# One branch at the end in place of two, one-pass group norms, and a layer that starts on half of the images, in a four-layer fp32 network on one core

## The chip, the core and the metric

The kernel runs on one core of a Trainium2 chip, in one launch. The metric is the device time of a launch in microseconds (us), as the median over several runs. TensorE is written PE, VectorE DVE, ScalarE ACT, GpSimd POOL and SyncE SP, as in the profile.

## The reference

The input x has 8 images of 384 channels and 32x32 pixels, all in fp32. Four layers follow each other, each of the form x + f(gn(x)), where gn is a group norm with 32 groups of 12 channels and without weights:

```python
def _gn(v, G=32, eps=1e-5):
    g = v.reshape(B_, G, C_ // G, H_, W_)
    m = jnp.mean(g, axis=(2, 3, 4), keepdims=True)
    s = jnp.var(g, axis=(2, 3, 4), keepdims=True)
    return ((g - m) / jnp.sqrt(s + eps)).reshape(v.shape)
...
# layer 0: q, k, v = 1x1 projection(gelu(batch norm(3x3 depthwise(x))))
attn = softmax(einsum('bhcn,bhcm->bhnm', q, k) * scale)        # 8 heads of 48 channels
out = bn(einsum('oc,bchw->bohw', w_out, einsum('bhnm,bhcm->bhcn', attn, v)))
# layer 1: 4 experts
scores = softmax(x_flat @ gate_w + gate_b, -1)
top_v, top_i = jax.lax.top_k(scores, K)                        # K = 2
top_w = softmax(top_v, -1)
present = (top_i[:, :, None] == jnp.arange(e)[None, None, :]).any(0)
coef = einsum('ke,kbhw->ebhw', present, top_w)
hdn = relu(einsum('bchw,edc->ebdhw', x, w1) + b1)
out = einsum('ebohw,ebhw->bohw', einsum('ebdhw,eod->ebohw', hdn, w2) + b2, coef)
# layer 2: 7x7 depthwise convolution with reflected edges, plus bias
# layer 3: three branches of small MLPs and 1x1, 3x3, 5x5 depthwise convolutions,
#          weighted by a softmax over pooled features, then a 384x384 projection
```

`present` says whether an expert was chosen by any pixel of any image at all, once as first and once as second choice. Where every expert was, coef is the same for all experts at a pixel: the two softmax weights add up to 1, so layer 1 is the plain sum over all four experts.

## The kernel before

**Tiles.** Channels lie on the 128 partitions in three tiles (NC = 3, "ct" 0 to 2); an image has N = 1024 pixels, in two halves of HF = 512, and each half in two of QF = 256. A matmul in fp32 appears in the trace as two instructions. A group norm over 12 channels crosses partitions: `over_group` (L237) multiplies the moments per channel with block matrices gmat, 7 of them (each output tile gets shares from its neighbouring tiles). `gn_steps` does this twice: the mean first, then DVE centres (L248 to L251), then the variance; `rsqrt` (L204, L205) raises to the power -0.5 on POOL, and L255 makes the offset. Scale and offset are applied by ACT (L270).

**Stages.** First layer 0's norm, convolutions, batch norms and projections; then attention, image by image (`attention`, scores L655, exponentials L662, output L674, projection L730). The kernel uses exponentials without subtracting a maximum, and notes in `shift_needed` whether a bound on the scores was exceeded. After it comes a branch (L845, L846): if so, `attention(True)` does all again with a maximum. All engines wait for it.

Then `bn_coefs` (L276 to L280) and the moments of layer 0's sum (L865 to L881), worked out from those of its parts without reading the sum, and the norm of all 8 images at once (L237 on 24 columns). s1, t1 (L883, L884) are kept.

**Layer 1** is `experts()`. Image 0's residual r is loaded (L1002, from layer 0's output in DRAM; L1003 the input xr), as are w1, one transfer per expert (L1030), and w2; DVE makes r (L1009), ACT normalises (L270, `normed`). For each image and half, 12 pairs of expert and hidden tile: three matmuls (L1147) and relu on ACT (L1151). Then the product with w2, in a scheme that trades matmuls for additions: `sums` (L1064) on DVE, 24 products of four experts each (L1071), whose results DVE adds to r (L1085, L1087). During the next image's first half the pieces of `next_layer` run, one every expert or two: the finished r is saved (L918, eight transfers on SP), its statistics taken (L210, L266), `gn_steps`, and for each ct `pass_on`: ACT normalises, DVE transposes (L902), POOL adds the mirrored edges (L903, L904) and SP saves (L928). `logits` (L1114, L1125) and the choice of experts go between too, and the last of it, `absent`, decides a second branch (L1371, L1372): `experts_by_token` would do layer 1 again with the choice per pixel. `attention` and layers 2 and 3 have their order on PE, ACT, DVE written out by hand (`manual_schedule`); in `experts()` a scheduler sets it. SP's transfers are placed by the scheduler everywhere.

**Layer 2** treats a depthwise 7x7 convolution as banded 64x64 matmuls over columns, with the images side by side (L1619): for each ct eight c, for each c two e (parities), each with 28 matmuls over all 8 images (64x256). Its weights are loaded (`load_weights`, L1344), their edges folded by POOL (L1348) and spread by ACT into a banded form (`next_weights`, L1361). xt, the transposed input of one ct for all images, is loaded ahead: ct 0 of images 0 to 6 at the end of `experts()`, ct 1 at L1449; image 7's ct 0 goes straight into it. After a pair of c, ACT takes the results from PSUM (L310). Layer 3 (L1586 and on) ends with the projection (L2001 to L2012), DVE's sum with the residual (L2016) and the output's transfers (L2023).

**Memory.** Pools are stacks: what is opened after a closing lies where the closed pool lay, and its first writers wait for the old pool's last users. Before, `wp` (gate weights) lies below `zs` (moments of the batch norm); `ew` (weights of layer 1) and then `er` (r, transposed tiles) come where zs was.

Of the kernel before, what the change touches and what calls it, by code (L numbers as in the profile page):

```python
# [18 lines left out]
P = 128  # L19
# [117 lines left out]
def conv_mixer_kernel(ctx: ExitStack, tc: tile.TileContext, a: dict, out: bass.AP):  # L137
# [79 lines left out]
    def gn_steps(mv, pool_ps, tag="gn", order="A"):  # L217
# [34 lines left out]
        yield  # L252
# [5 lines left out]
        yield s, t  # L258

# [34 lines left out]
    mvx = early.tile([P, 2, NC, B], FP, name="mvx")  # L294
    s1, t1 = (early.tile([P, NC, B], FP, name=f"{n}1") for n in "st")
# [20 lines left out]
    with (  # L316
# [27 lines left out]
        with tc.tile_pool(name="cps", bufs=2, space=PSUM, reuse_waits="tile") as cps:  # L344
# [70 lines left out]
            for n, (ct, v, u) in enumerate(groups):  # L415
# [21 lines left out]
                if n == 1:  # L437
                    norm = gn_steps((mvx[:, 0], mvx[:, 1]), slot0)
                    next(norm)
# [35 lines left out]
    wpool = ExitStack()  # L475
    wp = wpool.enter_context(tc.tile_pool(name="wp", bufs=1))
    zpool = ExitStack()
    zs = zpool.enter_context(tc.tile_pool(name="zs", bufs=1))
    zst = zs.tile([P, NC, 2 * B, 6], FP, name="zst")
    mvz = zs.tile([P, 2, NC, 2 * B], FP, name="mvz")  # L480
    mvxh = zs.tile([P, 2, NC, 2 * B], FP, name="mvxh")
    zx = zs.tile([P, NC, 2 * B], FP, name="zx")
    bn_gbo = load(zs, "bn_gbo")
    shift_needed = zs.tile([1, 1], mybir.dt.int32, name="shift_needed")

    def attention(shifted):

        with tc.tile_pool(name="aw", reuse_waits="tile", bufs=1) as aw, tc.tile_pool(  # L490
            name="ay", reuse_waits="tile", bufs=2
        ) as ay, tc.tile_pool(
            name="sc", reuse_waits="tile", bufs=3, space=PSUM
        ) as scp, tc.tile_pool(name="av", reuse_waits="tile", bufs=2, space=PSUM) as avp:
            pw_v = load(aw, "pw_v")
            w_out = load(aw, "w_out")
            if shifted:

                pws = pp0.tile([P, 2 * NC * NC, P], FP, tag="pw", name="pws")
                pw_q = pws[:, : NC * NP].rearrange("p (c k) n -> p c k n", k=NP)  # L500
                nc.sync.dma_start(out=pw_q, in_=a["pw_qs"])
                pw_k = load(aw, "pw_ks")
                ones_row = aw.tile([P, 1], FP, name="ones_row")
                nc.gpsimd.memset(ones_row, 0.0)
                nc.gpsimd.memset(ones_row[0:1, :], 1.0)
                nc.gpsimd.memset(ones_row[64:65, :], 1.0)
            else:
                pw_q, pw_k = pw[:, 0], pw[:, 1]

                own = aw.tile([P, 3], FP, name="own")
                nc.gpsimd.memset(own, 1.0)
                for o, base, sign in ((1, 15, -1), (2, -16, 1)):
                    for q in range(4):
                        v = own[32 * q : 32 * q + 32, o : o + 1]
                        nc.gpsimd.affine_select(
                            out=v, in_=v, compare_op=ALU.is_ge, fill=0.0, base=base,
                            pattern=[[0, 1]], channel_multiplier=sign,
                        )  # L520
                nc.gpsimd.tensor_copy(own[32:64, 0:1], own[32:64, 1:2])
                nc.gpsimd.tensor_copy(own[64:96, 0:1], own[64:96, 2:3])
            chk = aw.tile([P, B * 2 * NP], FP, name="chk")
            if shifted:
                mx = pws[:, NC * NP : NC * NP + 4]
                nc.gpsimd.memset(mx, 0.0)
            ys, kTs, qTs, atts, xs = {}, {}, {}, {}, {}

            def fetch(b):
                ys[b] = []  # L530
                for v in range(3):
                    if b == 0 and v in ys0 and not shifted:
                        ys[b].append(ys0[v])
                        continue
                    pool = pp0 if v < 2 else ay
                    y = pool.tile([P, NC, N], FP, tag=f"y{v}", name=f"y{v}", bufs=1)
                    nc.sync.dma_start(out=y, in_=raw[v][b])
                    ys[b].append(y)

            def activate(b, v):  # L540
                for ct in range(NC):
                    i = v * NC + ct
                    y = ys[b][v][:, ct, :]
                    affine(y, y, bn_s[:, i : i + 1], bn_t[:, i : i + 1], AF.Gelu)

            def two_banks():
                return scp.tile([P, 2, HF], FP, tag="sc", name="sc")

            def project(w, pair, y):
                ps = two_banks()  # L550
                for h in range(2):
                    for ct in range(NC):
                        nc.tensor.matmul(  # L553
                            ps[:, h, :], lhsT=w[:, ct, pair, :],
                            rhs=y[:, ct, h * HF : (h + 1) * HF],
                            start=ct == 0, stop=ct == NC - 1,
                        )
                return ps.rearrange("p h n -> p (h n)")

            def spread(w, y, o, own, act=False, between=None):  # L560


                for t in range(NC):
                    ps = project(w, t, y)
                    if between and t == NC - 1:
                        between()
                    to = [[(0, None)], [(32, 1), (64, 2)], [(96, None)]][t]
                    affine(o[:, t, :], ps, own[:, 0:1] if own is not None else 1.0, 0.0)
                    moves = [(o[64:96, t, :], 32, 2)]
                    moves += [(o[p : p + 32, NP - 1, :], 64, i) for p, i in to]  # L570
                    for d, p, i in moves:
                        if act:
                            nc.scalar.copy(d, ps[p : p + 32, :])
                        elif own is None or i is None:
                            nc.vector.tensor_copy(d, ps[p : p + 32, :])
                        else:
                            nc.vector.tensor_scalar(
                                d, ps[p : p + 32, :], own[p : p + 32, i : i + 1], None, ALU.mult
                            )

            def project_k(b):
                kT = kTs[b] = ay.tile([P, NP, N], FP, tag="kT", name="kT", bufs=1)
                if not shifted:
                    return spread(pw_k, ys[b][1], kT, None, b == 0)
                for pair in range(NP):
                    affine(kT[:, pair, :], project(pw_k, pair, ys[b][1]), 1.0, ones_row)

            def project_q(b, between=None):
                qT = qTs[b] = ay.tile([P, NP, N], FP, tag="qT", name="qT", bufs=1)
                if not shifted:  # L590
                    return spread(pw_q, ys[b][0], qT, own, between=between)
                for pair in range(NP):
                    ps = project(pw_q, pair, ys[b][0])
                    nc.vector.tensor_scalar(qT[:, pair, :], ps, HD**-0.5, None, ALU.mult)

            vTs = []

            def project_v(b):
                y = ys[b][2]
                if not vTs:  # L600
                    vTs.append(ay.tile([P, N // P, HEADS * 64], FP, tag="vT", name="vT", bufs=1))
                    nc.gpsimd.memset(vTs[0], 1.0)
                vT = vTs[0]
                for m0 in range(0, N // P, 2):
                    ps = two_banks()
                    for m in range(2):
                        for ct in range(NC):
                            nc.tensor.matmul(  # L608
                                ps[:, m, :C], lhsT=y[:, ct, (m0 + m) * P : (m0 + m + 1) * P],
                                rhs=pw_v[:, ct, :], start=ct == 0, stop=ct == NC - 1,  # L610
                            )
                    nc.vector.tensor_copy(
                        vT[:, m0 : m0 + 2, :].rearrange("p m (a c) -> p m a c", c=4)[:, :, :, 0:3],
                        ps[:, :, :C].rearrange("p m (a c) -> p m a c", c=3),
                    )

            def shift(b):

                qT, kT = qTs[b], kTs[b]
                for h in range(2):  # L620
                    for pair in range(NP):
                        for n in range(4):
# [24 lines left out]

            def scores(b, h, pair, g):

                es = []  # L650
                for m in range(g * GM, (g + 1) * GM):
                    sc = two_banks()
                    for s in range(2):
# [1520 lines left out]
```

## Time and profile before

| | us |
|---|---|
| median of 3 runs | 3244.41 (3243.41 to 3246.69) |
| profiled execution | 3250.0 |
| its span | 3248.1 |
| PE busy | 3048.7 |
| DVE busy | 1674.7 |
| ACT busy | 1189.1 |
| POOL busy | 257.9 |
| mean granted PE clock | 0.974 of full speed |

The profile is of one execution; its times are from the start of its span. In a row of a group the columns are: source line, engine, operation, what is written and from what, shape and count, then busy time, mean duration of one in ns, and the engine's idle time before them with what ended most of it. "PEld" is PE's weight load, which overlaps its matmuls; "SPq" and "DVEq" are an engine's own queue, as at a branch. Slices show an engine's busy share of 1/40 of the span in tenths. A timeline line has start, duration, engine, source line, operation, count, and in brackets the idle time ahead of it and what ended it; equal neighbours are drawn together. The rows of the page that cost most PE time are attention and layer 1:

```profile
L1147 PE MATMUL ph<-xn,w 128*128 128x512 f32 x1152 | 507.8, 597 | 0.7 <-ACT xn L270 0.7
L655 PE MATMUL sc<-qT,kT 64*128 64x512 f32 x2048 | 477.6, 603 | 10.4 <-ACT e L662 10.4
L674 PE MATMUL av<-e,vT 128*64 128x512 f32 x2048 | 467.7, 598 | 0.0
```

### The profile page before, as it was taken

The numbers are of one execution on the slowest core, as the hardware profiler recorded it, in microseconds if no ns is written. First come the engines' busy times: TensorE is split into PE (matmuls) and PEld (weight loads), VectorE is DVE, ScalarE is ACT, GpSimd is POOL, SyncE is SP. The second block draws the span as 40 slices with busy tenths as digits, with TensorE's granted clock in tenths as the row PEclk, the third lists the DMA queues.
The fourth block names the chain that finished last, engine by engine and source line by source line (L and its number), as shares of the span: only waits on it lengthen the run. The fifth ranks groups of instructions, "written<-read, shape, count | busy, mean of one in ns | idle before, by whom it ended". The sixth has DMA issues, their size and how long they took to land. (4 is left out here: it accounts for less than half of the span.)

```text
span 3248.1 us, 42048 instructions
## 1 busy us (share of the span) xinstructions
PE 3048.7 (94%) x17628; PEld 1615.6 (50%) x17628; DVE 1674.7 (52%) x2536; ACT 1189.1 (37%) x1340; POOL 257.9 (8%) x408
## 2 busy tenths in 40 slices
PE   5987999999999999999997999999999997987999
PEld 3774334343433333343432576676666665655544
DVE  6996344445444544444444454553654654257174
ACT  3644553535354453535442212212212111446520
POOL 3331000000000000000002100000000000111400
PEclk9998999999999999999998999999999997998999
DMA  5887001011101111020014021121121113777665
GB/s 215 288 277 263 36 31 71 23 61 42 61 22 59 43 40 61 22 80 23 13 35 153 14 57 44 62 75 34 55 82 28 42 43 105 276 258 237 224 219 198
DMA packets 87992, 322.76 MB, mean 99 GB/s; under 512 B 13304, under 2 KB 15696, under 8 KB 83560
## 3 DMA queue, kind: packets, MB, share of 16 engines
q1 hardware_dynamic: 64168, 251.71, 22.7%
q10 hardware_dynamic: 13488, 35.81, 3.5%
q0 software_dynamic: 10128, 32.36, 2.9%
q8 instruction: 143, 2.34, 0.3%
q14 instruction: 65, 0.53, 0.1%
HBM read 211.65 MB, written 111.53 MB: 99 GB/s over the span
## 5 line engine op out<-in xcount | busy, mean ns | idle before, releaser
L662 ACT ACTIVATE e<-sc 128x1024 f32<-128x1024 f32 x512 | 483.1, 1029 | 544.0 <-PE sc L655 543.6
L1147 PE MATMUL ph<-xn,w 128*128 128x512 f32 x1152 | 507.8, 597 | 0.7 <-ACT xn L270 0.7
L655 PE MATMUL sc<-qT,kT 64*128 64x512 f32 x2048 | 477.6, 603 | 10.4 <-ACT e L662 10.4
L674 PE MATMUL av<-e,vT 128*64 128x512 f32 x2048 | 467.7, 598 | 0.0
L1151 ACT ACTIVATE hs<-ph,b 128x512 f32<-128x512 f32 x192 | 131.9, 687 | 605.6 <-PE ph L1147 552.7
L1147 PEld LDWEIGHTS ph<-xn,w 128*128 128x128 f32 x1152 | 217.3, 191 | 260.8 <-issue 256.7
L655 PEld LDWEIGHTS sc<-qT,kT 64*128 64x128 f32 x2048 | 185.7, 186 | 297.4 <-issue 228.9
L674 PEld LDWEIGHTS av<-e,vT 128*64 128x64 f32 x2048 | 135.5, 136 | 316.5 <-issue 316.5
L553 PE MATMUL sc<-y,pw 128*128 128x512 f32 x576 | 252.1, 599 | 8.0 <-ACT y L270 8.0
L425 PE MATMUL ps<-xt,wx 64*64 64x256 f32 x3456 | 198.2, 388 | 41.0 <-DVE xt L361 22.0
L690 DVE LOAD_MASK_SELECT sm<-av x64 | 0.9, 14 | 424.1 <-PE av L674 424.1
L692 DVE RECIPROCAL inv<-sm 128x512 f32<-128x512 f32 x64 | 214.6, 3353 | 2.2
L1085 DVE TENSOR_TENSOR r<-r,p 128x256 f32<-128x256 f32 x416 | 155.3, 416 | 104.0 <-PE p L1071 103.1
L425 PEld LDWEIGHTS ps<-xt,wx 64*64 64x64 f32 x3456 | 155.5, 137 | 82.6 <-issue 44.9
L1619 PE MATMUL ps<-xt,wx 64*64 64x256 f32 x2688 | 158.2, 394 | 30.7 <-SPq L1372 18.5
L553 PEld LDWEIGHTS sc<-y,pw 128*128 128x128 f32 x576 | 109.8, 192 | 149.8 <-issue 138.6
L1071 PE MATMUL p<-hs_sum,wsum 128*128 128x256 f32 x768 | 173.7, 379 | 0.5 <-DVE r L1085 0.5
L1064 DVE TENSOR_TENSOR hs_sum<-hs 128x768 f32<-128x768 f32 (+1 forms) x96 | 60.7, 687 | 206.9 <-ACT hs L1151 206.9
L1071 PEld LDWEIGHTS p<-hs_sum,wsum 128*128 128x128 f32 x768 | 145.8, 190 | 20.8 <-DVE r L1085 1.1
L1619 PEld LDWEIGHTS ps<-xt,wx 64*64 64x64 f32 x2688 | 109.4, 138 | 78.3 <-issue 26.0
L608 PE MATMUL sc<-pw_v,y 128*128 128x384 f32 x384 | 127.5, 493 | 13.0 <-ACT y L270 13.0
L1064 DVE TENSOR_TENSOR hs_sum<-hs,hs_sum 128x768 f32<-128x768 f32 (+1 forms) x192 | 138.2, 775 | 1.1
(302 smaller groups left out, 3322.6 us busy)
## 6 DMA issues: line engine op xcount, KB each, us to landing
raw<-y SPq DMA_DIRECT2D x72, 512.0 KB
y<-raw SPq DMA_DIRECT2D x24, 1536.0 KB
x<-x SPq DMA_DIRECT2D x23, 608.0 KB
xt<-x SPq DMA_DIRECT2D x23, 608.0 KB
w<-in_w ACTq DMA_DIRECT2D x36, 384.0 KB
xn<-in_x SPq DMA_DIRECT2D x24, 512.0 KB
x<-in_x SPq DMA_DIRECT2D x16, 768.0 KB
z<-z POOLq DMA_DIRECT2D x16, 768.0 KB, 4.3
```

Of the source, the lines that this page charges most:

```text
L425: nc.tensor.matmul(ps[64 * d : 64 * d + 64, 2 * i + e, cc], lhsT=w[r, 12 * cc + 6 * e + 3 * d + k, :], rhs=xt0s[ct][r, 16 * d + 4 * u + 2 ...
L553: nc.tensor.matmul(ps[:, h, :], lhsT=w[:, ct, pair, :], rhs=y[:, ct, h * HF : (h + 1) * HF], start=ct == 0, stop=ct == NC - 1,)
L655: nc.tensor.matmul(sc[:, s, :], lhsT=kTs[b][r, pair, m * P : (m + 1) * P], rhs=qTs[b][r, pair, h * HF : (h + 1) * HF], start=True, stop=True,)
L662: nc.scalar.activation(e, sc, AF.Exp, scale=1.0 if shifted else HD**-0.5)
L674: nc.tensor.matmul(av[64 * s : 64 * s + 64, :], lhsT=vTs[0][:, m, c0 : c0 + 64], rhs=e[:, s, :], start=m == 0, stop=m == N // P - 1,)
L692: nc.vector.reciprocal(inv, sm)
L1064: nc.vector.tensor_add(rows_of(o, hs, s), rows_of(i, hs, s), rows_of(j, hs, s))
L1071: nc.tensor.matmul(ps[:, :QF], lhsT=block(w)[:, e], rhs=rows_of(x, hs, e), start=e == 0, stop=e == E - 1,)
L1085: nc.vector.tensor_tensor(out=o, in0=o, in1=ps[:, :QF], op=op)
L1147: nc.tensor.matmul(ph, lhsT=w1[:, e, ct, dc * P : (dc + 1) * P], rhs=xns[b, h][:, ct, :], start=ct == 0, stop=ct == NC - 1,)
L1151: nc.scalar.activation(hs[:, dc, e], ph, AF.Relu, bias=b1[:, e, dc : dc + 1])
L1619: nc.tensor.matmul(ps[64 * d : 64 * d + 64, 2 * i + e, c % 2], lhsT=w[r, d * K7 + k, :], rhs=by_slot(xts[ct])[r, 16 * d + column(c, e, 2), ...
```

## The change

Everything behind layer 0's projections is put into a function `layers(again, ...)`. Both branches go. `bounded` (of attention) and the presence of the experts are multiplied into one flag `repeat`, and at the very end one branch calls `layers(True, ...)`, which does attention with the maximum and layer 1 per pixel, and all behind. For it, layer 0's statistics xst are saved to DRAM, and mvx and the group means of x (gmx) stay in a lasting pool.

A group norm of layers 1 and 2 no longer finds the mean before the variance. The group mean of its input is guessed from known numbers (`ref`: the mean of the layer's input plus a constant of the biases, gmy); DVE forms the moments about that reference, and one pass of 7 matmuls yields both. In layer 1's start the power is taken in two parts, image 0 first.

`experts()` now has its order written by hand, POOL included. The pool er is opened ahead of ew. Four weight tiles of layer 2 are spread at its end (a fourth, wx4, lies in er). Image 7's norm comes in two parts: moments of ct 0 and 1 and group block 0, then the rest. Between them PE does layer 2's c = 0 and 1 on images 0 to 3, and after them on images 4 to 7. PSUM's two tiles of four banks are one pool on each side.

```diff
+    def centred(o, mean, var, ref):
+        nc.vector.tensor_sub(o[:, :, 0], mean, ref)
+        nc.vector.tensor_mul(o[:, :, 1], o[:, :, 0], o[:, :, 0])
+        nc.vector.tensor_add(o[:, :, 1], o[:, :, 1], var)
+
+    def from_moments(own, ps, ref, s, t, gm, firsts=None):
+        c, n = ps.shape[1], ps.shape[3]
+        both, sq = (
+            own.tile([P, c, n], FP, tag=f"fm_{k}", name=f"fm_{k}") for k in "ab"
+        )
+        nc.vector.tensor_copy(both, ps[:, :, 0])
+        nc.vector.tensor_mul(sq, both, both)
+        nc.vector.scalar_tensor_tensor(
+            out=sq, in0=ps[:, :, 1], scalar=EPS, in1=sq, op0=ALU.add, op1=ALU.subtract
+        )
+        nc.vector.tensor_add(gm, both, ref)
+        for n0, n1 in firsts or ((0, n),):
...
+            nc.gpsimd.tensor_tensor(
+                out=s[:, :, n0:n1], in0=sq[:, :, n0:n1], in1=half, op=ALU.pow
+            )
+            nc.vector.scalar_tensor_tensor(
+                out=t[:, :, n0:n1], in0=gm[:, :, n0:n1], scalar=-1.0, in1=s[:, :, n0:n1],
+                op0=ALU.mult, op1=ALU.mult,
+            )
...
+                    nc.gpsimd.dma_start(out=xstmem, in_=xst)
+                    nc.vector.tensor_copy(gmx, next(norm))
...
     with tc.manual_schedule(engines=ORDERED):
-        attention(False)
-    gate_w = load(wp, "gate_w")
-    gate_b = load(wp, "gate_b")
-    redo = nc.values_load(shift_needed[:1, :1], min_val=0, max_val=1)
-    with tc.If(redo > 0):
-        attention(True)
+            attention(again)
...
-        s, t = gn_coefs((mr, vr), mg)
-        v.tensor_copy(s1, s)
-        v.tensor_copy(t1, t)
+            ref = zs.tile(shape, FP, name="ref")
+            dq = zs.tile([P, NC, 2, B], FP, name="dq")
+            v.tensor_add(ref, gmx, gmy[:, :, 0:1].to_broadcast(shape))
+            centred(dq, mr, vr, ref)
+            ps = mg.tile([P, NC, 2, B], FP, tag="gn", name="gn_ps")
+            over_groups(ps, dq, range(NC))
+            from_moments(zs, ps, ref, s1, t1, gm1, ((0, 1), (1, B)))
     zpool.close()
...
-    ew = ewpool.enter_context(tc.tile_pool(name="ew", bufs=1))
-    er = ewpool.enter_context(tc.tile_pool(name="er", bufs=2, reuse_waits="tile"))
...
+            er = erpool.enter_context(tc.tile_pool(name="er", bufs=2, reuse_waits="tile"))
...
+            ew = ewpool.enter_context(tc.tile_pool(name="ew", bufs=1))
...
         def next_layer(b):
             r = rs[b]
+                parts = (range(NC),) if b < B - 1 else (range(2), range(2, NC))
+                cos = (range(NC),) if b < B - 1 else (range(1), range(1, NC))
+                for i, (cts, co) in enumerate(zip(parts, cos)):
+                    if i == len(parts) - 1:
             keep_residual(r, b)
-            mv = image_stats(r)
+                    moments2(r, b, cts, mv, dq)
             yield
-            norm = gn_steps(mv, eh, "sm")
-            next(norm)
+                    ps = eh.tile([P, NC, 2, 1], FP, tag=("sm", "pl")[i], name="gn_ps")
+                    over_groups(ps, dq, co)
             yield
-            s, t = next(norm)
+                    norm2(ps, b, co, st)
             yield
...
-            nc.vector.tensor_scalar(absent, least[:1], 0.5, None, ALU.is_lt)
+                nc.vector.tensor_mul(least[:1], least[:1], bounded)
+                nc.vector.tensor_scalar(repeat, least[:1], 0.5, None, ALU.is_lt)
...
+            for _ in range(4):
         next_weights()
-        for _ in passing:
-            pass
+            return passing
...
-    redo = nc.values_load(absent[:1, :1], min_val=0, max_val=1)
-    with tc.If(redo > 0):
+            if again:
         experts_by_token()
...
+            ps0 = four_banks().rearrange("p i (c b h) -> p i c b h", b=B, h=H)
+            begun = {}
+            for c in range(2):
+                for e in range(2):
+                    w = begun[c, e] = weights.pop((K7, 0, c, e))
+                    convolve7(ps0, 0, c, e, w, slice(0, HB))
+                for _ in range(4 if c == 0 else B):
+                    next(last, None)
+            for c, e in product(range(2), repeat=2):
+                convolve7(ps0, 0, c, e, begun.pop((c, e)), slice(HB, B))
+                if (c, e) != (1, 1):
+                    next_weights()
+        erpool.close()
+        ehpool.close()
...
+    layers(False, early, xst, pre_pool, pp0, pw)
+    redo = nc.values_load(repeat[:1, :1], min_val=0, max_val=1)
+    with tc.If(redo > 0):
...
+        layers(True, early, xst, pre_pool, pp0, None)
```

`over_groups` is the seven matmuls of `over_group` on both moments at once; `convolve7` is the loop of L1619 for a range of images; `four_banks` hands out the two PSUM tiles in turn. The diff ignores indentation.

## The prediction

> **What bounds the kernel now.** I read the page's busy shares first, then its 40 slices, then the chain of waits by line, then the timeline and tables by stretch around the places that the change touches.
>
> ```profile
> PE 3048.7 (94%) x17628; PEld 1615.6 (50%) x17628; DVE 1674.7 (52%) x2536; ACT 1189.1 (37%) x1340; POOL 257.9 (8%) x408
> ...
> PE   5987999999999999999997999999999997987999
> ...
> L1619 PE MATMUL ps<-xt,wx 64*64 64x256 f32 x2688 | 158.2, 394 | 30.7 <-SPq L1372 18.5
> L1071 PE MATMUL p<-hs_sum,wsum 128*128 128x256 f32 x768 | 173.7, 379 | 0.5 <-DVE r L1085 0.5
> ```
>
> TensorE is the bound nearly everywhere. One slice is 81.2 us; the dips at the 22nd and the 34th are the ends of layer 0 and of layer 1, where something ends late and PE starves. The row of L1619 names the second dip: 18.5 us before the 7x7 convolution are put down to the branch at L1372. The row of L1071 says that layer 1's products waited 0.5 us in all for DVE's adds.
>
> The table over layer 1 (columns: stretch, length, busy time of PE, weight loads, DVE, ACT, POOL, clock, DMA share, GB/s) shows that inside it PE never waits, 2.3 us in 947:
>
> ```profile
> 1780.76:2727.46 946.70, 944.37 (x3454) 609.99 (x3454) 496.41 (x985) 191.64 (x265) 33.80 (x59) 1.00 0.17 52
> ```
>
> So there only removed PE work can gain, and any wait that is added costs in full. The timeline (start, duration, engine) of the first boundary:
>
> ```profile
> 1752.32 1.48 DVE L276 BATCH_NORM_AGGREGATE bn_mv<-zst 128x2 f32<-128x96 f32 x3 [3.35 <-DVEq L846]
> 1752.43 0.34 SPq L1002 DMA_DIRECT2D r<-z  x1
> ...
> 1756.32 3.13 PE L237 MATMUL gn_ps<-mom,gmatA 128*128 128x8 f32 x14 [12.04 <-DVE mom L878]
> ...
> 1760.45 3.15 PE L237 MATMUL gn_ps<-gn_d,gmatA 128*128 128x8 f32 x14 [1.00 <-DVE gn_d L251]
> ...
> 1763.90 4.16 POOL L205 TENSOR_TENSOR gn_s<-ve,mhalf 128x24 f32<-128x24 f32 x1 [2.54 <-DVE ve L204]
> ...
> 1780.76 1.55 PE L1147 MATMUL ph<-xn,w 128*128 128x512 f32 x3 [0.67 <-ACT xn L270]
> ```
>
> The norm is ready at 1768.3, but the steady stream of PE starts at 1780.76, when the third channel tile of image 0's residual has landed: loads, not the norm, end this boundary. The second boundary, and a norm inside layer 1:
>
> ```profile
> 2729.94 3.39 PE L237 MATMUL gn_ps<-gn_mv,gmatA 128*128 128x1 f32 x14 [2.48 <-DVE gn_mv L266]
> ...
> 2734.26 3.12 PE L237 MATMUL gn_ps<-gn_d,gmatA 128*128 128x1 f32 x14 [0.94 <-DVE gn_d L251]
> ...
> 2750.71 0.34 SPq L928 DMA_DIRECT2D x<-x  x1
> 2755.84 20.79 PE L1619 MATMUL ps<-xt,wx 64*64 64x256 f32 x336 [18.47 <-SPq L1372]
> ...
> 2780.51 19.87 PE L1619 MATMUL ps<-xt,wx 64*64 64x256 f32 x327 [3.87 <-ACT wx L1361]
> ```
>
> ```profile
> 1899.93 1.62 PE L237 MATMUL gn_ps<-gn_mv,gmatA 128*128 128x1 f32 x14
> 1901.41 2.82 PE L1147 MATMUL ph<-xn,w 128*128 128x512 f32 x6
> ```
>
> PE's last product ends at 2727.46, and apart from 6.5 us of norm matmuls nothing runs on it until 2755.84. The x14 shows that each of the 7 fp32 matmuls of a mean is recorded as two.
>
> [...] 14 norm matmuls take 3.13 us after the idle stretch, 1.62 us inside layer 1. [...] DVE waits 3.35 us at L846, and from SP's last issue (2750.71) to PE's restart behind L1372 are 5.1 us. [...] between 1765 and 1775 the table shows a DMA share of 1.02.
>
> **The change, part by part.**
>
> *Layer 0.* The copy of xst to DRAM (147 KB on POOL's queue), one copy of 24 columns on DVE and the constants of the known reference on POOL lie beside attention: 0 to 1 us, taken 0.5.
>
> *Start of layer 1.* Gone are the branch (3.35 us idle on DVE) and one norm's round trip: 3.13 us of PE and about 1 us of DVE. Added are three DVE operations for the centred moments, at 0.17 us. Chain: DVE begins at 1752.32-3.35 = 1748.97; moments 4.0 us as before; centring 0.6; norm matmuls 3.1; four DVE operations 0.8; then POOL's power in two parts, image 0 first (0.88 us, as in the 128x3 row), then 21 columns (4.16x21/24 = 3.6 us). The norm ends near 1763.1 instead of 1768.3. But er, which holds the residual r, is now allocated ahead of ew and lies where zs lay; zs also holds ref, dq and the temporaries of the one-pass norm. So image 0's first load of r waits for POOL's second power: from 1752.43 it goes to about 1763. SP issues in order: the first two input tiles and w1 of experts 0 to 2 stand ahead of the load and go out by 1750, w1 of the last expert, w2 and the third tiles stand behind it and wait with it. Before, 4.72 MB of weights and 1.05 MB of tiles from 1760.96 had landed at 1777.6: 347 GB/s. Now 5.05 MB from 1763.1 land at 1777.7. Thus the third tile is normalised near 1780.7 as before, while PE has done only two instead of four logical matmuls ahead (+1.7), [...] and the gating of image 0 no longer lies in the gap (+0.9): **+4 us**, range -3 (r lands early after all) to +8 (two more transfers of 1.5 us late). The 5 us of the chain are hidden behind the loads.
>
> *Images 0 to 6.* Each norm loses 14 recorded matmuls: 1901.41-1899.93 = 1.48 us of a full PE, seven times **-10.4 us**. What hides its DVE part: six matmuls stood between the two before, and pieces of the norm still lie one expert apart. The hand-written order of layer 1 (before: the scheduler's) puts all bn_stats at the image's end and the last two sums five adds later. DVE is busy 496 of 947 us, and a sum is needed only one product later; cost 0, bounded by 0 and 1 us per image.
>
> *Layer 2's start.* After: PE's products end at 2727.5; the weights of c=0,1 are loaded and spread during the last products, since ACT is free. c=0 on four images: 80 recorded 64x128 matmuls took 11.01 us later in the trace, so 112 of them 3.85 (2728.6 to 2732.5). Part one of image 7's norm (1.6 us), c=1 on four images (3.85), then PE waits for DVE: transposing ct 0 (1.98 us) stands there before part two's moments; part two's matmuls at about 2741. The second half of c=0,1 ends at 2750.8 (7.7 us[...]), c=2 at 2757. Then c=3 needs a weight tile that ACT spreads, and ahead of that on ACT is the eviction of c=0,1, whose output waits for the last save of image 7 on a DMA lane: until about 2761. c=3 ends near 2764.2. Before: c=3 begins at 2780.51; the table of ten-us stretches has 184 of its matmuls between 2760 and 2770, so its 112 take 6.1, with 1.6 of small waits 2788.3. Difference 24; **-23 us** taken: -17 if the eviction waits 6 us longer, -26 if it doesn't wait. The halves cost PE 15.4 instead of 12.3 us (contained). The eight saves of image 7's residual (6.65 us of issuing on SP, at 2728.60 before) move into part two, ahead of the saves of its second and third tile; only the eviction above hangs on them. The second channel tile's loads are issued near 2755 (before: 2758.31), land near 2772 at the rate above and are needed when c=7 is done, near 2789: hidden by 17 us.
>
> *End.* All engines now take one branch behind the last work. Before, the last output lands at the end of the span, some 5 us after DVE's last result; the branch (3.4 to 5.1 us above) lies beside that landing, or comes after it: 0 to +5, taken +2.
>
> Sum: 0.5+4-10.4-23+2 = **-27 us**. The profiled execution took 3250.0 (span 3248.1), so 3223; it lies 5.6 over the median of the runs, 3244.4, which thus becomes **3217**.
>
> **Rivals.**
> - *Layer 2 is held by its loads (A).* The four early weight tiles, the saves of image 7 and the second channel tile share engines that are full from 2760 (share 0.98). For it: L1619's row already waits 11.9 us for spread weights. Against: four tiles are spread ahead of the layer where two were. Then only about 10 us of that boundary stay: -14, 3230.
> - *The first boundary gains too (C).* If r's first tiles come before the weights, its 5 us and the branch show: -38, near 3206.
> - *Layer 1's written order starves PE (B), slower.* Place: product 8 of each half, where the next product waits for hs_sum on DVE behind adds and, at image ends, behind 1.9 us of bn_stats. It decides from 27/16 = 1.7 us per half. At 2.6 us (two sums and three bn_stats) in all 16 halves it is +42, in sum +15: 3259. Against: PE waited 0.5 us in all for DVE's adds, and adds keep pace with PE.
> - *The redo is taken (D)*: attention and all behind it twice, over +2000 us. In the trace of before no instruction of either branch ran, so the joint condition should be false.
>
> **Numbers.** -27 as reckoned (-39 to -13): 0.64. C: 0.08. A: 0.14. B: 0.12, two thirds of it slower, the rest near no change. D: 0.02. A measurement of this kernel tells 0.2%, 6.5 us, from no change. Faster: 0.64+0.08+0.12 from A+0.01 = 0.85; same: 0.02 from A and 0.03 from B; slower: 0.08+0.02. Known costs give -39 to -13 (3205 to 3231); to hold the greater part of A and C the range is 3203 to 3237.
>
> **What would show it.** In the trace after: r's first load near 1763, not 1752; PE's stream in layer 1 starting near 1781[...]; one norm row per image inside layer 1, and that stretch still over 99% busy; 64x128 convolutions from about 2728.6, with an idle stretch of some 2 us ahead of the second half; c=3 done some 37 us after the last product (before: 61); at the end, a branch beside the last output's landing. Wrong would be: idle PE inside the products, a wait of more than 6 us for spread weights or the eviction, or a second attention.

## The result, and the profile after

The changed kernel takes 3271.75 us (median of 4 runs, 3265.67 to 3273.21) against 3243.91 of the kernel before (4 runs): ratio 1.0083, 95% interval 1.0066 to 1.0101. It is slower by 28 us, where 27 us less were forecast. The profiled execution has a span of 3263.7 us.

The two timelines, cut at the same eight points, give the length of each stage (us; from the first start, or to the last end, of the matmuls named):

| stage | before | after | difference |
|---|---|---|---|
| start to the first projection of layer 0 | 283.4 | 280.1 | -3.3 |
| to the first score matmul | 64.1 | 55.5 | -8.6 |
| attention, to its last matmul | 1396.8 | 1396.8 | 0 |
| to the first product with w2 | 64.2 | 70.9 | +6.7 |
| layer 1, to its last product | 918.9 | 929.3 | +10.4 |
| to layer 3's first matmul | 210.6 | 197.8 | -12.8 |
| to the output projection | 172.2 | 194.2 | +22.0 |
| to DVE's last result | 132.7 | 131.9 | -0.8 |
| to the end of the span | 5.2 | 7.2 | +2.0 |

The differences add up to 15.6 us, not to 28: of the two executions that were profiled, that of before (3250.0 us) lies 6 us above its kernel's median and that of after (3265.67) 6 us below. Against two more profiles of the kernel before (runs 11 and 12, spans 3239.0 and 3236.8) the span after is 24.7 and 26.9 us longer; layer 1 then loses 12.5, and the stage to layer 3's first matmul gains 8.6 to 11.7.

The first row scatters from 276.6 to 285.8 over 14 profiles of both kinds and says nothing. Two rows carry most of the loss: layer 3 and layer 1. The groups by line of the kernel after (busy us and mean ns, then PE's idle time ahead and who ended it):

```profile
L1267 PE MATMUL ph<-xn,w 128*128 128x512 f32 x1152 | 508.1, 599 | 20.6 <-ACT xn L308 20.6
L1168 PE MATMUL p<-hs,wsum 128*128 128x256 f32 x256 | 59.7, 382 | 12.0 <-DVE r L1184 12.0
L1716 PE MATMUL ps<-xt,wx 64*64 64x256 f32 x1024 | 68.1, 424 | 12.2 <-ACT o L352 12.2
```

The 20.6 us at L1267 belong to layer 1's start. The wait at L1168 is new. That at L1716 is not wholly so: before, these convolutions waited 8.8 us for ACT, all at one place (L1586 at 3091.34), and now four times 1.8 to 3.5. Over layer 1, from the first product with w2 to the last, PE was idle for 2.3 us of 918.9 before; the table by stretch now shows it idle for 21 us:

```profile
1803.28:2732.60 929.32, 908.24 (x3309) 587.45 (x3307) 503.76 (x990) 187.62 (x264) 31.49 (x61) 0.99 0.17 53
```

**Layer 3.** The table over the stage to the output projection, before and after:

```profile
2938.00:3110.30 172.30, 140.60 (x2201) 93.09 (x2201) 74.38 (x131) 97.58 (x153) 44.26 (x101) 0.89 0.69 227
2930.40:3124.60 194.20, 149.85 (x2200) 98.28 (x2200) 74.51 (x131) 97.75 (x153) 44.07 (x101) 0.86 0.62 202
```

Of the 22 us, PE is idle for 12.7 more and busy for 9.2 more, at a lower mean clock (0.86 instead of 0.89). The timeline after, at the 5x5 convolutions (L1716) and the hidden rows (L1916):

```profile
3018.19 4.62 PE L1716 MATMUL ps<-xt,wx 64*64 64x256 f32 x80
3024.37 1.84 ACT L352 COPY o<-ps 128x2048 f32<-128x2048 f32 x1
3026.27 7.25 PE L1716 MATMUL ps<-xt,wx 64*64 64x256 f32 x80 [3.45 <-ACT o L352]
3033.45 7.09 PE L1916 MATMUL ps<-y,mw1s 128*72 128x512 f32 x16
3040.46 4.62 PE L1716 MATMUL ps<-xt,wx 64*64 64x256 f32 x80
```

and the same place before:

```profile
3017.93 9.00 PE L1586 MATMUL ps<-xt,wx 64*64 64x256 f32 x160
3024.11 1.84 ACT L310 COPY o<-ps 128x2048 f32<-128x2048 f32 x1
3026.86 7.09 PE L1789 MATMUL ps<-y,mw1s 128*72 128x512 f32 x16
```

A group of convolutions is two times 80 recorded matmuls, with the hidden rows between the first 80 and the second. Before, the next group's 80 follow at once (x160); after, they wait until ACT has emptied the group just finished, and then run in 7.25 us, not 4.62. One cycle takes 22.3 us (3018.19 to 3040.46) instead of 15.95 (3017.93 to 3033.88). It is the dearest of three: behind the next two waits, of 3.50 us each, the 80 matmuls take 6.26 and 5.93 us.

**Layer 1.** DVE's timeline after, in the second image's first half, with the PE line that waits for it:

```profile
1909.88 1.98 DVE L957 STREAM_TRANSPOSE x<-xn 128x1024 f32<-128x1024 f32 x1 [3.57 <-DMA x<-x]
1915.42 1.98 DVE L957 STREAM_TRANSPOSE x<-xn 128x1024 f32<-128x1024 f32 x1 [3.57 <-DMA x<-x]
1917.25 2.85 DVE L1161 TENSOR_TENSOR hs_sum<-hs 128x768 f32<-128x768 f32 x3
...
1928.03 0.87 DVE L1184 SCALAR_TENSOR_TENSOR r<-r,badd,p 128x256 f32<-128x256 f32 x2
```

```profile
1928.95 1.35 PE L1168 MATMUL p<-hs,wsum 128*128 128x256 f32 x5 [1.58 <-DVE r L1184]
...
2686.12 0.57 PE L1028 MATMUL pp<-anyp,ones 128*128 128x8 f32 x2 [9.12 <-DVE anyp L1024]
```

The third transpose waits on DVE for the save of its buffer, the sums stand behind it in the written order, the additions behind the sums, and PE's products run out of PSUM: 1.6 to 2.1 us, once per image, seven times. And in the last half image PE stands 9.1 us in front of the small matmul of the expert choice (L1028), where it stood 1.8 us before (L973).

**Layer 1's start**, the timeline after:

```profile
1733.20 0.73 POOL L886 DMA_DIRECT2D z<-z  x1 [43.96 <-ACT z L885]
...
1741.40 0.20 POOL L1145 MEMSET ones<- 128x128 f32 x1 [7.47 <-PE pm L264]
1741.57 0.89 POOL L205 TENSOR_TENSOR zn_s<-ve,mhalf 128x3 f32<-128x3 f32 x1
...
1748.76 4.49 POOL L290 TENSOR_TENSOR s<-fm_b,mhalf 128x3 f32<-128x3 f32 x2 [6.31 <-DVE fm_b L283]
...
1753.28 0.81 SPq L1096 DMA_DIRECT2D r<-z  x2
```

The first load of r is issued at 1753.28, when the second power ends, as forecast, and SP's next transfer behind it, one of w, at 1754.13. POOL's power for the batch norm stands behind a memset that starts only at 1741.40: in the built program it waits, among others, for the save of layer 0's last tile, issued at 1733.20. The bracket names PE's small norm (pm), which has nothing to do with these bytes; it was only the last event that the profile saw.

**Layer 0** gained, in a place the forecast did not look at. Before, and after:

```profile
326.91 1.23 ACT L1361 ACTIVATE wx<-w,parity 128x448 f32<-128x448 f32 x2 [13.64 <-POOL w L1348]
...
330.32 4.03 PE L608 MATMUL sc<-pw_v,y 128*128 128x384 f32 x7 [13.00 <-ACT y L270]
```

```profile
317.07 3.50 ACT L308 ACTIVATE y<-y,bn_t,bn_s 128x1024 f32<-128x1024 f32 x3 [6.06 <-DMA y<-raw]
318.37 4.09 PE L668 MATMUL sc<-pw_v,y 128*128 128x384 f32 x7 [5.17 <-ACT y L308]
```

L1361 is the spreading of layer 2's first weights. The scheduler had moved it to 327 us, ahead of attention, where ACT waited 13.6 us for those weights with v's activations behind it. In the changed kernel it lies in the written order of layer 1, and ACT waits 6.1 us at that place, for a load. From the first projection to attention it is 63.0 to 64.1 us in four profiles with the old order, 55.5 to 57.3 in ten with the new one. That the moved instruction makes the whole difference was not tried by itself.

### The profile page after: what moved, and what is told of

Same layout as the page of the kernel before. It is cut to its first block, busy times and chain, and to the rows that moved or that the text cites. A ratio compares the mean times of both kernels' runs of the same rounds, so it can differ in the third digit from the quotient of the medians.

```text
span 3263.7 us, 42215 instructions
## 1 busy us (share of the span) xinstructions
PE 3046.0 (93%) x17740; PEld 1606.7 (49%) x17740; DVE 1694.3 (52%) x2566; ACT 1186.5 (36%) x1340; POOL 264.5 (8%) x415
## 4 chain that ended last, share of the span: by engine, by line
PE 72%; DVE 11%; DMA 7%; issue 6%; ACT 3%; POOL 1%; ACTq 0%; SPq 0%; DVEq 0%; POOLq 0%
PE av L734 13%; PE sc L715 13%; PE p L1168 11%; PE ph L1267 11%; PE sc L613 7%; PE sc L668 4%; PE sc L790 3%; DVE hs_sum L1161 2%; DMA w<-in_w 2%; DVE stats L210 2%; DVE y L436 2%; PE ps L1716 2%; PE ps L1045 1%; DMA r<-r 1%; DMA x<-x 1%
## 5 line engine op out<-in xcount | busy, mean ns | idle before, releaser
L1267 PE MATMUL ph<-xn,w 128*128 128x512 f32 x1152 | 508.1, 599 | 20.6 <-ACT xn L308 20.6
L715 PE MATMUL sc<-qT,kT 64*128 64x512 f32 x2048 | 477.6, 603 | 10.4 <-ACT e L722 10.4
L1267 PEld LDWEIGHTS ph<-xn,w 128*128 128x128 f32 x1152 | 218.7, 192 | 284.9 <-issue 256.2
L715 PEld LDWEIGHTS sc<-qT,kT 64*128 64x128 f32 x2048 | 185.6, 186 | 297.5 <-issue 228.7
L467 PE MATMUL ps<-xt,wx 64*64 64x256 f32 x3456 | 196.7, 386 | 39.3 <-DVE xt L403 21.9
L1045 PE MATMUL ps<-xt,wx 64*64 64x256 f32 (+1 forms) x2912 | 163.8, 384 | 23.2 <-ACT wx L1471 13.5
L1168 PE MATMUL p<-hs_sum,wsum 128*128 128x256 f32 x768 | 173.6, 379 | 0.0
L1168 PEld LDWEIGHTS p<-hs_sum,wsum 128*128 128x128 f32 x768 | 145.9, 190 | 19.8
L1161 DVE TENSOR_TENSOR hs_sum<-hs,hs_sum 128x768 f32<-128x768 f32 (+1 forms) x192 | 147.3, 781 | 5.0
L352 ACT COPY o<-ps 128x2048 f32<-128x2048 f32 x56 | 103.8, 1855 | 74.7 <-PE ps L467 30.6
```

The costliest lines, as they stand in the source:

```text
L467: nc.tensor.matmul(ps[64 * d : 64 * d + 64, 2 * i + e, cc], lhsT=w[r, 12 * cc + 6 * e + 3 * d + k, :], rhs=xt0s[ct][r, 16 * d + 4 * u + 2 ...
L715: nc.tensor.matmul(sc[:, s, :], lhsT=kTs[b][r, pair, m * P : (m + 1) * P], rhs=qTs[b][r, pair, h * HF : (h + 1) * HF], start=True, stop=True,)
L1045: nc.tensor.matmul(ps[64 * d : 64 * d + 64, 2 * i + e, c % 2, images], lhsT=w[r, d * K7 + k, :], rhs=by_slot(xts[ct])[r, 16 * d + column(c ...
L1161: nc.vector.tensor_add(rows_of(o, hs, s), rows_of(i, hs, s), rows_of(j, hs, s))
L1168: nc.tensor.matmul(ps[:, :QF], lhsT=block(w)[:, e], rhs=rows_of(x, hs, e), start=e == 0, stop=e == E - 1,)
L1267: nc.tensor.matmul(ph, lhsT=w1[:, e, ct, dc * P : (dc + 1) * P], rhs=xns[b, h][:, ct, :], start=ct == 0, stop=ct == NC - 1,)
```

## The experiments

Stage lengths and medians of all kernels (us; columns as in the table above; ratio to the kernel before):

| kernel | to first product | layer 1 | to layer 3 | to projection | median | ratio, interval |
|---|---|---|---|---|---|---|
| before | 64.2 | 918.9 | 210.6 | 172.2 | 3243.91 | |
| after | 70.9 | 929.3 | 197.8 | 194.2 | 3271.75 | 1.0083 (1.0066 to 1.0101) |
| 1 PSUM order | 70.5 | 930.8 | 194.0 | 171.0 | 3238.99 | 0.9984 (0.9976 to 0.9991) |
| 2 choice | 70.8 | 924.2 | 197.0 | 197.6 | 3262.20 | 1.0055 (1.0041 to 1.0069) |
| 3 third tile | 71.6 | 915.8 | 194.2 | 197.7 | 3251.39 | 1.0020 (1.0009 to 1.0032) |
| 4 start | 61.6 | 929.5 | 192.3 | 196.5 | 3259.41 | 1.0050 (1.0036 to 1.0064) |
| 5 before, strict turn | 64.3 | 916.8 | 209.3 | 199.5 | 3274.15 | 1.0094 (1.0077 to 1.0111) |
| 6 four mends | 61.1 | 904.4 | 192.6 | 168.2 | 3203.51 | 0.9877 (0.9858 to 0.9896) |
| 7 bias tile | 60.7 | 904.4 | 191.3 | 172.2 | 3205.32 | 0.9883 (0.9867 to 0.9898) |
| 8 no end branch | 61.3 | 904.4 | 191.6 | 174.9 | 3199.64 | 0.9864 (0.9849 to 0.9880) |
| 9 all images | 61.2 | 904.4 | 192.1 | 171.7 | 3202.97 | 0.9870 (0.9855 to 0.9885) |
| 10 ones only | 68.2 | 929.3 | 194.6 | 197.8 | 3266.80 | 1.0071 (1.0057 to 1.0085) |

Where no cause acts, a stage still differs by up to 2 us in layer 1 and some 4 us behind it (three profiles of the kernel before: 206.4 to 210.6 and 170.9 to 175.0).

**1. The PSUM order.** The changed kernel takes its two tiles of four banks strictly in turn. In the built programs the 5x5 groups among the hidden rows all have banks 0 to 3 and the hidden rows always 4 to 7; in the kernel before, whose pool of two buffers gives out the one that is free, consecutive groups alternate. The cut with `units` is of the hidden rows, the one below it of the branches' means.

```diff
-turns = iter((True, False))
+turns = iter((False, False))
...
-pb = banks().tile([MR, B])
+pb = banks(False).tile([MR, B])
...
-slot, units = banks(), []
+slot, units = banks(i == 0), []
...
-slot = banks()
+slot = banks(False)
...
-pg = banks().tile([P, NC, 3, B])
+pg = banks(False).tile([P, NC, 3, B])
```

> The changed kernel with the two PSUM tiles handed out so that each small or hidden tile takes the one that the running convolution does not hold, and the next convolution group follows it there (the order of the kernel before); nothing else. Theory (the strict turn lets consecutive 5x5 groups of layer 3 fall on the same four banks, so that each waits for ACT's eviction of the last): layer 3 from its first 64x128 matmul to its last DVE result goes from 326 us back to about 305, the 3.5 us waits on ACT at L1716 vanish, and the whole is about 21 us faster than the changed kernel: 3250. Rival (layer 3 is late because its loads and weights come from busier queues): the waits move to weights or DMAs and the gain is under 5 us: 3267 to 3272.

Measured: 3238.99, 33 us less than the changed kernel. The two profiles lie 23.7 us apart, and 23.2 of it is the stage to the projection. (The stage ahead of layer 3 is 3.8 us shorter, but that is no more than its scatter: runs 3, 4 and 10, which keep the strict turn, have 192.3 to 194.6 there.) The timeline of this run:

```profile
3012.87 9.00 PE L1716 MATMUL ps<-xt,wx 64*64 64x256 f32 x160
3019.05 1.84 ACT L352 COPY o<-ps 128x2048 f32<-128x2048 f32 x1
3021.81 7.09 PE L1916 MATMUL ps<-y,mw1s 128*72 128x512 f32 x16
```

The x160 is back, and eviction lies beside PE's work again. The rival falls.

**5. The same part alone, in the kernel before:** its pool split in two that are taken in turn.

```diff
-tp = pspool.enter_context(tc.tile_pool(name="tp", bufs=2, space=PSUM, reuse_waits="tile"))
+tps = [pspool.enter_context(tc.tile_pool(name=n, bufs=1, ...)) for n in ("tpl", "tpr")]
...
+def four_banks(turn=True):
+    ps = tps[len(taken) % 2].tile([P, 4, HF], FP, tag="ps", name="ps")
...
```

> The kernel before, its PSUM pool of two buffers replaced by two pools of one that are handed out in strict turn, as in the changed kernel; nothing else. Theory (the strict turn alone makes layer 3 late): about 26 us slower than the kernel before, 3270, with the 3.5 us waits on ACT in the 5x5 stage and one more ahead of layer 2's last group. Rival (it hurts only beside the other loads of the changed kernel): under 10 us slower.

Measured: 3274.15 against 3244.34, 30 us slower. The stage to the projection takes 199.5 us, against 170.9 to 175.0 in three profiles of the kernel before:

```profile
3020.43 4.62 PE L1595 MATMUL ps<-xt,wx 64*64 64x256 f32 x80
3026.60 1.84 ACT L310 COPY o<-ps 128x2048 f32<-128x2048 f32 x1
3028.50 6.16 PE L1595 MATMUL ps<-xt,wx 64*64 64x256 f32 x80 [3.44 <-ACT o L310]
```

So this one edit is worth the whole loss of 28 us; all the rest of the change came out 5 us faster (run 1). The stage ahead of layer 3, 209.3 us, is not longer than before (206.4 to 210.6).

**2. The expert choice.** `any_chosen`'s matmul six expert steps later (k = 10 of the last half instead of 4).

```diff
-present = any_chosen(chosen(lg, gtile), gtile, ones, eh)
+at = chosen(lg, gtile)
+yield
+present = any_chosen(at, gtile, ones, eh)
...
-if h == 1 and k in (0, 1, 2, 4):
+if h == 1 and k in (0, 1, 2, 4, 10):
```

> The changed kernel with the matmul that asks whether an expert was chosen (L1028) six expert steps later in PE's order of the last half image. Theory (the written order puts it behind a DVE chain that is not yet done, so that PE stands for 9.1 us): the wait of 9.1 us vanishes, about 9 us faster than the changed kernel: 3263. Rival (PE catches up at layer 2's start, which waits for image 7's loads and saves anyway): the wait vanishes, but layer 2's c=3 ends at the same time; 3269 to 3272.

Measured: 3262.20; layer 1 is 5.1 us shorter, not 9, since a wait of 4.3 us is left: the two reductions ahead of the matmul had moved with it behind the sums on DVE. The medians differ by 9.5 us, but their intervals overlap, so the size is not settled by this run. In run 6 the reductions stay at k = 4, and no wait is left.

**3. The third tile.**

```diff
-if h == 0 and passing and k in (0, 2, 3, 4, 6, 8):
+if h == 0 and passing and k in (0, 2, 3, 4, 6):
     next(passing)
...
 if k == 9:
     sums(hs, HSUMS[:-2], slice(0, E - 1))
+    if h == 0 and passing:
+        next(passing)
```

> The changed kernel with the third tile of each image's pass to the next layer behind the first sums of the half image instead of ahead of them. Theory (DVE runs in the written order, its third transpose waits 7.2 us for the save of the second tile's buffer, and the sums queue behind it until the products of PE run out of PSUM): the seven waits of 1.6 to 2.1 us at L1168 go, 12 us in sum, 3260; the transposes wait no longer. Rival (DVE's own work is too much for the stretch): the waits stay or move to other products, gain under 3 us.

Measured: 3251.39, 20 us less; layer 1 is 13.5 us shorter and the seven waits are gone. The other 6 us of the difference are not seen in the stages: the two profiles lie only 7.3 us apart.

**4 and 10. The start of layer 1.** In run 4 four things move to the pool `early`, in run 10 only the last of them.

```diff
-ref = zs.tile(shape, FP, name="ref")
+ref = early.tile(shape, FP, name="ref")
-dq = zs.tile([P, NC, 2, B], FP, name="dq")
+dq = early.tile([P, NC, 2, B], FP, name="dq0")
...
-from_moments(zs, ps, ref, s1, t1, gm1, ((0, 1), (1, B)))
+from_moments(early, ps, ref, s1, t1, gm1, ((0, 1), (1, B)))
...
-ones = ew.tile([P, P], FP, name="ones")
+ones = early.tile([P, P], FP, name="ones_e")
```

> The changed kernel with the norm's reference, its moments and temporaries and the matrix of ones in the pool that lasts through layer 1 instead of in memory that image 0's residual or layer 0's last tiles take. Theory (the residual's loads wait for POOL's second power, which itself stands behind a memset that waits for layer 0's last save): the first load of r is issued about 9 us after attention's last matmul instead of 21, the steady stream of PE in layer 1 starts some 8 us sooner after attention: 3264. Rival (the bandwidth for the weights of layer 1 ends this boundary, whatever the order): the load is early, but the stream starts less than 3 us sooner: 3269 or more.

> The changed kernel with only the matrix of ones moved to the lasting pool; the norm's temporaries stay where the residual lands. Theory (two causes at layer 1's start: 3.4 us of POOL's memset behind layer 0's last save, and the residual behind POOL's second power): the norm and r's first load come 3.4 us sooner after attention, r still behind the power, and the first product comes 3 to 4 us sooner. Rival (the memset alone makes it all late): 9 us sooner, as with both moved.

Measured: from attention to the first product 61.6 us with all moved, 68.2 with the ones alone, 70.9 with none; medians 3259.41, 3266.80, 3271.75. So the memset costs 2.7 us, a little less than expected, and the residual's place 6.6. In run 4 the load and PE's stream stand so:

```profile
1746.38 0.80 SPq L1096 DMA_DIRECT2D r<-z  x2
...
1765.70 31.31 PE L1267 MATMUL ph<-xn,w 128*128 128x512 f32 x68 [4.10 <-ACT xn L308]
```

11 us after attention's last matmul (1735.3) instead of 21, and the stream 30.4 us after it instead of 40.0. So the bandwidth for the weights did not end this boundary, though the rival and the forecast had it so.

**6. Four mends together** (the choice with its reductions ahead).

> The changed kernel with the four mends together (PSUM order, matmul of the expert choice later and its DVE part ahead, third tile behind the sums, norm and ones in the lasting pool). Theory (the four losses are separate places on PE's path): the gains add up; by the stage lengths of the four profiles 26+9+14+9 = 58 us less than the changed kernel, some 3214 and 30 us faster than the kernel before, close to what was forecast for the change. Rival (they hide each other): 3230 or more.

Measured: 3203.51, 1.2% faster than the kernel before. The table by stretch over its layer 1:

```profile
1795.57:2699.99 904.42, 904.30 (x3309) 586.82 (x3307) 503.90 (x990) 187.49 (x264) 22.64 (x61) 1.00 0.18 55
```

PE is idle for 0.1 us of 904: with the waits gone, layer 1 shows the forecast's 10.4 us of removed norm matmuls (PE is busy for 914.6 us of this stage in runs 11 and 12, and for 904.3 here), and 2.3 us of small waits of the kernel before are gone as well (918.9 - 904.4 = 14.5; the rest is within the 2 us of scatter).

**7. The bias tile.** `po = banks(False)...` in place of `po = banks()...`.

> As the one with four mends, and the small tile of the output bias takes the four banks that the next convolution group gets, so that this group does not wait for the eviction of the last but one (a wait of 5 to 9 us at that place in the kernel before too). Theory: 5 us less than with four mends, 3209. Rival (the stage behind waits for layer 3's hidden rows from DRAM or for the bias instead): no difference over 2 us.

Measured: 3205.32, no gain. The wait changed its name and did not get shorter (for ACT's eviction it was 2.44 us in run 6, 5.02 in run 1):

```profile
3043.99 10.08 PE L1722 MATMUL ps<-xt,wx 64*64 64x256 f32 x144 [9.14 <-DVE obias L2043]
```

Now the group waits for DVE to have read the bias tile. The theory of this run falls.

**8. Without the branch at the end.**

> As the one before it, without the branch at the end and the redo behind it: the case that some expert is chosen nowhere or a score is out of bounds is left out of the computation. Theory (the branch follows the last output's landing by 2 us): 2 us less than with the branch, the end from DVE's last result 5.2 us instead of 7.2. Rival (the branch lies beside the landing): no difference.

Measured: 3199.64; from DVE's last result to the end 5.1 us, with the branch 7.1. The medians differ by more (5.7), but their intervals overlap.

**9. Layer 2 on all images at once.**

```diff
-    convolve7(ps0, 0, c, e, w, slice(0, HB))
...
-convolve7(ps0, 0, c, e, begun.pop((c, e)), slice(HB, B))
+convolve7(ps0, 0, c, e, begun.pop((c, e)), slice(0, B))
```

> The kernel with four mends, but layer 2 begins on all 8 images at once, behind the whole norm of image 7; nothing else. Theory (most of the gain at layer 2's start is the branch that is gone and the shorter norm; the half start only lays 7 us of matmuls beside the norm and costs 3 for the smaller tiles): 4 to 6 us slower than with four mends, 3208 to 3210. Rival (the half start carries that gain): 15 us or more slower.

Measured: 3202.97, the same as with the half start, where 5 us more were expected. The timelines show why; with the half start (run 6):

```profile
2701.21 3.32 PE L1046 MATMUL ps<-xt,wx 64*64 64x128 f32 x112 [1.22 <-issue]
...
2735.52 55.34 PE L1046 MATMUL ps<-xt,wx 64*64 64x256 f32 x952 [5.97 <-ACT wx L1477]
```

and without (run 9):

```profile
2716.49 75.85 PE L1046 MATMUL ps<-xt,wx 64*64 64x256 f32 x1344
```

Counted from layer 1's last product (2699.99 and 2702.65), PE starts 12.6 us sooner with halves, then runs into the spreading of the fourth c's weights. That stands on ACT behind the eviction of c=0 and 1 (L352 at 2732.48), which waited 9.61 us for a DMA, the save of a transposed tile (x<-x), as the forecast had it. Without halves PE stands during the norm and then goes through 1344 matmuls. The ends of these runs of matmuls lie 90.9 and 89.7 us behind layer 1's last product.

**11 and 12. The kernel before, for layer 0.**

> The kernel before, unchanged, for another profile of layer 0. In the profiles so far attention begins at 347.5 and 344.9 us with layer 0 as before, at 334 to 342 in ten with the changed one. Theory (scatter between executions, since layer 0's work is the same but for one copy and one save): it begins anywhere between 334 and 348. Rival (the change moved something in layer 0 that gains some 8 us): at 343 to 348 again.

> As the run before it, once more: the theory of scatter expects a start of attention between 334 and 348, the rival 343 to 348.

Measured: attention starts at 343.6 and 340.6 (one execution each, of 3240.72 and 3238.64 us). The start alone does not tell the two apart, but the stretch from the first projection does (63.0 and 64.0 us, in the result above): scatter lies ahead of it, a constant 7 us in it.

## Why the prediction was wrong

- **The step that failed most was not in the sum.** The two PSUM tiles, "one pool on each side" in the description of the change, got no line among its parts, and layer 3 no term: both were put at nothing, without a reason. Each group of convolutions then waited for ACT to empty the one before it, which cost 22 us in layer 3. Runs 1 and 5 show this from both sides: 33 us less without the strict turn, 30 us more with nothing else. It was there to be seen: `banks()` is called between the matmuls of one group.
- **"Images 0 to 6", the cover.** The -10.4 us for the norm matmuls were right (run 6). The cover of the written order was costed at "0, bounded by 0 and 1 us per image": it was 1.7 us per image, 12.0 in all, and 9.1 for the expert choice (1.8 before), which this step did not name. Behind the 9.1 us the granted clock was 0.50 (2686.12 to 2690.00), and over layer 1 PE is busy 3.9 us longer than in run 6. Run 3 shows the first; for the second, run 2 shows that the wait shrinks as the matmul moves, run 6 that it goes. Rival B had the mechanism (sums late on DVE, PE out of products) but another place: it looked at the sums and bn_stats, not at the transposes and their saves ahead of them, and at each half where it is once an image.
- **Layer 1's start.** +4 with a range of -3 to +8 (what it holds beyond +1.7 and +0.9 was an estimate of the author's); measured +6.7. PE's first products there ran at a granted clock of 0.50 (1772.42 to 1775.60), the next at 1.00 (1775.70 to 1780.00). That it fell into the range is luck in part. That r waits for POOL's second power was right (it ends at 1753.25). The memset was not in it (2.7 us), and the assumption that bandwidth ends this boundary anyway was wrong: run 4 wins 9.3 us there.
- **Layer 2's start.** -23 forecast, in a range of -26 to -17. By the end of the run of matmuls that starts at 2780.51 before (57.18 us long) and at 2769.22 after (53.95), counted from the last product (2727.46 and 2732.63): 110.2 and 90.5, so -19.7. The profile of before was late here, though: the same matmuls end at 105.9 and 106.3 in runs 11 and 12, which leaves -15.4 and -15.8. The wait that the forecast put at the end of its chain is there: ACT empties c=0,1 only 33.6 us after the last product (L352 at 2766.18; 33.5 were reckoned). But c=3 ends 41.4 us after it, not 37: the spreading stands behind that eviction on ACT, and PE restarts at 2769.22 with a mean clock of 0.55 up to 2772.70. The time put down for the second half of c=0,1 beyond 7.7 us of matmuls was an estimate of the author's, and c=3 did not hang on it; from 2745.10 to 2751.80, in that half, the granted clock was 0.50. The half start has no part in the gain (run 9). What remains is what the gone branch, the shorter norm and the early weights give together; these were not tried apart. 6.9 us were given back up to layer 3, and no run shows by what.
- **End.** +2 was taken from between 0 and +5; +2.0 was measured. Run 8 shows which case it was: the branch comes after the landing (5.1 us from DVE's last result to the end without it, 7.1 with it).
- **Layer 0.** 0.5 forecast, -8.6 measured, most likely by an instruction of layer 2 that the scheduler no longer moves ahead of attention. No run tried this alone; the timelines of 14 profiles agree.
- **The other rivals.** C did not come: the first boundary lost 6.7 us. A (-14) is near the lower figures for layer 2's start, but the full engines that it rests on did not come: the DMA share is 0.73 from 2750 to 2760 and from 2760 to 2770, where it was 0.98 in the second of these before. D did not come: the scores (L715) are recorded 2048 times, as before (L655).
- **Two slips, worth some 1 us at most.** The 64x128 matmuls that took 11.01 us are 320 in the trace, not 80; the 3.85 us for 112 of them are reckoned with 320. The chain at layer 1's start adds up to 1762.0 from the terms given, not to 1763.1.

Without the strict turn the forecast's sign would have been right (run 1, -5 us), its size not.

## What to carry to other kernels

A buffer handed out in strict turn is only equal to a pool of two if no short-lived tile is taken between the parts of a long-lived one; count the takes, and let the short one use what the next long one will get, if it is emptied soon (run 7's was not: 9.14 us of waiting for DVE). The strict turn cost 33 us by run 1 and 30 by run 5. When a scheduler's order is replaced by a written one, look on each engine for an instruction that waits for a DMA, and at what stands behind it (run 3: layer 1 13.5 us shorter). Work laid beside a wait wins nothing if the next thing it needs (here spread weights) comes no sooner (run 9: 3202.97 us against 3203.51).

## What the runs showed of the hardware

The wait of 3.45 us that ends at 3026.27 in the changed kernel cost PE more than itself: the 80 matmuls behind it took 7.25 us, the same 80 without it 4.62, so this cycle lost 6.3 and the next one, with 3.50 and 6.26, 5.4. The granted clock was 1.00 ahead of the wait (3019.00 to 3022.80), 0.50 from 3026.27 to 3030.00 and 1.00 again from 3033.50. The waits of 1.6 to 2.1 us in layer 1 of the changed kernel had no such tail (8 matmuls in 1.99 us against 1.89, and a granted clock of 1.00 from 1780 to 2677). Behind layer 1 of the same execution, waits of such a length had one: behind that of 2.08 us, which ends at 2837.12, the clock was 0.50 from 2837.20 to 2840.50, and behind that of 1.76 us, which ends at 3105.52, it was 0.50 from 3106.90 to 3110.20. So in these traces the length of one wait does not by itself tell what clock PE gets behind it.
